# The normed tile of the second pass: turned by VectorE after a trip through memory, two units later

## The chip, the cores and the metric

The kernel runs on one core of a Trainium2 chip. A core has five engines with instruction queues of their own: TensorE (PE; its weight loads are shown apart, as PEld), VectorE (DVE), ScalarE (ACT), GpSimd (POOL) and SyncE (SP), which here only issues DMAs. Each queue is worked off in order; between queues there are semaphores. The metric is device time in microseconds (us); the profile is one execution of the same program, recorded by the hardware.

## The reference, cut to what matters

Two layers follow one another on an input of 8 images of 32 x 32 positions and 512 channels (f32). The first is a group norm, an attention over 1024 positions with 8 heads, and a residual. The second one is a deformable attention: a layer norm, a strided 7 x 7 depthwise convolution that gives sampling positions, 256 bilinear samples of the image as keys and values, attention of all 1024 queries over them, and then, for each position:

```python
msa = att @ mo_w + mo_b
z = msa + x.reshape(b, h * w, c)
z_ln = layernorm(z, ln_g, ln_b)
out = jax.nn.gelu(z_ln @ mlp_w + mlp_b, approximate=False) + z
```

The change concerns `z_ln @ mlp_w`. TensorE multiplies along the partition axis, so the normed tile, which has positions on the partitions, has to be turned until the channels lie there.

## The kernel before, in words

The program has two passes. The first does the first layer, the first layer norm and most convolutions; it ends near 2160 us of the profile. The second pass (`with ExitStack() as l1`) works in 64 units: `2 * B * NHP`, that is 16 half images `hi` (512 positions each) by 4 pairs of heads. Unit `n` computes the scores of its pair (`sc`), their maxima (`nmax`, VectorE), exponentials (`e`, ScalarE), turns `e` in blocks of 32 x 32 on VectorE (`sq`) and brings it to the form of `et` by a write to memory and a read; `att.product` (`av`) follows one unit later and `attH` holds the scaled result. `query_step` makes the queries of the next unit from `hat` (`hat_h`).

`back_steps(hi, start, step)` is the rest of a half image, as four tiles `t` of 128 positions, one tile per unit, in the units after the attention of that half. For each tile:

- `fetch`, `add` (per pair of tiles): read `xr` from `mid` (SP) and add `bo_row` (GpSimd)
- `joined`: product with `wo`, sum `z`, its mean and variance `mv` (VectorE; the power -1/2 on GpSimd, in `rstd`)
- `norm`: `zn`, VectorE
- `turned`: four 128 x 128 transposes on TensorE into PSUM, copied to `zT` by ScalarE in two halves
- `mlp`: product with `wm`, `zT` as weights; `biased`: `res`, VectorE
- `gelu` (ScalarE) and `end` (GpSimd: add `z`, write out), for two tiles together

The order is written out by hand: `at(place, step)` puts a step on a list, `run_due` runs the list in order of `place`, and `InOrder` keeps every engine's instructions in that order. The place is a unit and a fraction: 0 is the scores; 0.02 and 0.04 the two `sq` transposes with their writes; 0.0401 to 0.0411 the reads of `et` and `inv`; 0.042 the next queries; 1.1 and 1.2 `av` and `attH`. With `n` the unit of a tile, `turned` stood at n + 0.6, after the `av` of the unit before; `mlp` at n + 1.03, and the last steps of a pair at 1.72 and 2.24 behind its second tile.

Between these lie the remaining convolutions (`conv_steps`): lane 0 on VectorE (5 or 3 taps per unit), lane 1 on ScalarE and GpSimd (7 taps per unit: `parts`, then `chunk`), with `fill` products on TensorE. `point_steps(b)` turns the result of image `b` into positions (`targets`), gathers four rows per half (GpSimd, `row`, four buffers) and weighs them (`sample`, VectorE, `smp`), then makes keys and values of the image (`mm<-smp,wC`, `mm<-wB,smp`). With `NHP = 4` an image takes eight units.

Where the passes meet, `prep` loads `hat` twice, `lng` and `lnb` (`load_small`), repeats two vectors (`rep_w`, VectorE), gathers and samples image 0, loads the weights (`load_late`) and makes the first queries, keys and values. `rows` and `scaled` fold `lnb` and `lng` into `bm_row` and `wm`. DMAs of SP and of ScalarE take eight semaphores in turn; a DMA is issued when the eighth before it has landed.

Of the kernel before, what the change touches and what calls it, by code (L numbers as in the profile page):

```python
# [17 lines left out]
P = 128  # L18
# [229 lines left out]
def attention_then_deformable_attention(  # L248
# [131 lines left out]
    def at(place, step):  # L380
        due.append((place, len(due), step))
# [671 lines left out]
    with ExitStack() as l1:  # L1053
# [15 lines left out]
        def load_small():  # L1069
            with nc.allow_non_contiguous_dma(reason="small vectors onto partitions"):  # L1070
                for t, v in ((lng, ln_g), (lnb, ln_b)):
                    nc.sync.dma_start(t, v.rearrange("(c p) -> p c", p=P))

        def load_conv():
            nc.sync.dma_start(dww, dw_w.rearrange("(c p) a u v -> p c (a u v)", p=P))
# [94 lines left out]
        def fetch_hat(hi):  # L1170
            hat[hi] = raw.tile([P, NC, C], F32, tag="hat", name="hat_h", bufs=2)
            nc.sync.dma_start(hat[hi], hat_d[hi // 2][:, ts(hi % 2, NC), :])

# [29 lines left out]
        def back_steps(hi, start, step, tail=False):  # L1203
# [6 lines left out]

            def fetch(t):
                xr[t] = tmp("xr", 4)
                nc.sync.dma_start(xr[t], xs[t])

            def add(t):
                nc.gpsimd.tensor_tensor(xr[t], xr[t], bo_row, ALU.add)
# [9 lines left out]
                rstd(mv[:, 2:3], mv[:, 1:2], 1e-5)  # L1226

            def norm(t):
                zn[t], mv = tmp("zn", 2), xr["mv", t]
                nc.vector.tensor_scalar(  # L1230
                    zn[t], z[t], mv[:, 0:1], mv[:, 2:3], ALU.subtract, ALU.mult
                )

            def turned(t):
                ps = mm_tile()
                for c in range(NC):
                    nc.tensor.transpose(ps[:, ts(c, P)], zn[t][:, ts(c, P)], ident)
                zT[t] = tmp("zT", 2)
# [17 lines left out]
            for t in range(NC):  # L1256
                over, eve = (start + step * t >= n_units - i and not tail for i in range(2))
                n, pair = start + step * t, start + step * (t - t % 2)

                ends = (n + 0.6, n + 1.03, n + 1.0392)  # L1260
                if eve:
                    ends = (n + 0.61, n + 0.72, n + 0.73) if over else (n + 1.06, n + 1.62, n + 1.625)
                places = (pair - 1.6, pair - 0.5), (n + 0.012, n + 0.03), ends
                if tail:
                    turn = n + 0.15 + 0.005 * (t > 0)
                    places = (n - 0.7, n - 0.6), (n, n + 0.01), (turn, n + 0.25, n + 0.26)
                steps = (fetch, add), (joined, norm), (turned, mlp, biased)
                for place, what in zip(sum(places, ()), sum(steps, ())):
                    at(place, lambda t=t, what=what: what(t))


                ends = [t - 1, t] if t % 2 and not tail else [t] if tail else []

                for what, after in (
                    (gelu, 0.27 if tail else 0.735 if over else 1.72),
                    (end, 0.28 if tail else 0.74 if over else 2.24),
                ):
                    for i in ends:
                        at(n + after, lambda i=i, what=what: what(i))
# [33 lines left out]
        def conv_steps():  # L1313
            for lane, chunks in enumerate(((0, 3, 6), (1, 2, 4, 5, 7))):
                free = 0.5 + lane
                for k in chunks:
# [7 lines left out]
                    unit = int(fills[1]) + 1  # L1324
                    i = 0
                    while i < KS * KS:
                        points = unit % (2 * NHP) in (NHP - 1, NHP, NHP + 2)
                        count = 7 if lane else 3 if points else 5
                        for j in range(count):
                            if i == KS * KS:  # L1330
                                break
                            place = 0.25 + 0.01 * j if not lane else 0.045 + 0.001 * j if j < 4 else 0.65 + 0.01 * j
                            at(unit + place, lambda b=b, cb=cb, i=i, lane=lane: tap(b, cb, i, lane))
                            free = unit + place
                            i += 1
                        unit += 1

        def point_steps(b):
            last = 2 * NHP * b - NHP
            ready = last - (b == 1)  # L1340
            at(ready - 3.5, lambda: conv_load(b))
            at(ready - 2.035, lambda: conv_gelu(b))
            at(ready - 1.465, lambda: offsets(b))
            at(ready - 1.36, lambda: offsets_turned(b))
            at(ready - 0.959, lambda: targets(b))
            for h, (p0, p1) in enumerate(((-0.28, 0.0415), (1.72, 2.0415))):
                place = last if h else ready
                at(place + p0, lambda h=h: gather(b, h))
                at(place + p1, lambda h=h: sample(b, h))
# [6 lines left out]
        def load_late():  # L1356
            nonlocal bq_row, wo, wm, bo_row, bm_row, wq_r
            wo = load_w(late2, mo_w, "wo")
            wm = load_w(late2, mlp_w, "wm")
            bo_row = load_row(late, mo_b, "bo_row")  # L1360
            bm_row = load_row(late2, mlp_b, "bm_row")
            bq_row = load_row(wp, bq, "bq_row")
# [65 lines left out]
```

## Time and profile before

| | us |
|---|---|
| runs of the kernel before | 3321.34, 3324.23, 3326.19 (median 3324.23) |
| the profiled execution, own time | 3324.95 |
| its span, first to last instruction | 3323.3 |
| PE busy | 3263.3 (98%) |
| VectorE busy | 2494.1 (75%) |
| ScalarE busy | 1808.0 (54%) |
| GpSimd busy | 1540.5 (46%) |
| four transposes of zn, 64 times: PE busy | 41.9 |
| copies of zT, ScalarE busy | 41.0 |

All lines of the page have the line L54, a helper's, so work is told apart by tile names: `mm<-ident,zn` reads "writes mm, from ident and zn". A timeline row has the start, the duration, the engine, the operation, and in brackets how long the engine had been idle and what ended that. PE rows overlap by the pipeline, so a group's hold on PE is read from start to start. A table by stretches gives the busy time of each engine in a window. A list of waits gives who waited for whom, the total, the number of waits and the longest.

### The profile page before, as it was taken

What the parts mean: (1) busy time and instruction counts of PE and PEld (TensorE: products, weight loads), DVE (VectorE), ACT (ScalarE), POOL (GpSimd) and SP (SyncE); (2) the same over time, 40 slices, a digit from 0 to 9 for tenths busy, and PEclk for the clock granted to TensorE, in tenths of its full rate; (3) what the DMA queues carried; (4) which work ended last, traced back from release to release, by engine and by line L of the source; (5) the groups of instructions that cost most, each with busy time, mean ns of one, the idle gap of its engine ahead of it and who ended that gap; (6) DMA issues with size and microseconds to landing.
All of it is one profiled execution on the core that took longest, in us unless ns stands there. A gap on an engine that the chain in (4) does not pass through costs nothing.

```text
span 3323.3 us, 59497 instructions
## 1 busy us (share of the span) xinstructions
PE 3263.3 (98%) x21664; PEld 1323.2 (40%) x21664; DVE 2494.1 (75%) x3392; ACT 1808.0 (54%) x3918; POOL 1540.5 (46%) x1907
## 2 busy tenths in 40 slices
PE   8999999999999999999999999999999999999998
PEld 4344444444344344443444443333333333333333
DVE  5777777888898888888898787557767586665754
ACT  3443356576567567567567555145565565554442
POOL 1001316746755765664664663415555364641222
PEclk9999999999999999999999999999999999999999
DMA  5666766766767777776776776676666565675653
GB/s 151 178 178 164 210 179 186 217 190 177 220 192 185 207 201 186 204 196 179 211 199 171 201 214 189 178 240 211 198 197 214 175 214 187 202 231 191 214 182 130
DMA packets 442792, 643.62 MB, mean 194 GB/s; under 512 B 74274, under 2 KB 238114, under 8 KB 440452
## 3 DMA queue, kind: packets, MB, share of 16 engines
q1 hardware_dynamic: 409232, 531.93, 55.5%
q0 software_dynamic: 31632, 106.84, 10.6%
q8 instruction: 172, 2.82, 0.3%
q10 hardware_dynamic: 1636, 1.06, 0.1%
q14 instruction: 120, 0.98, 0.1%
HBM read 247.44 MB, written 123.74 MB: 112 GB/s over the span
## 4 chain that ended last, share of the span: by engine, by line
PE 88%; ACT 3%; DVE 3%; POOL 2%; DMA 1%; issue 1%; SPq 1%; another core or an unknown queue 0%; POOLq 0%; ACTq 0%; DVEq 0%
PE mm L54 55%; PE sc L54 17%; PE av L54 16%; ACT e L54 2%; SPq L54 1%; POOL chunk L54 1%; DVE nmax L54 1%; DVE smp L54 1%; DVE sq L54 1%; DMA et<-sq 0%; POOL xr L54 0%; POOL res L54 0%; ACT L54 0%; ACT parts L54 0%; DVE chunk L54 0%
## 5 line engine op out<-in xcount | busy, mean ns | idle before, releaser
L54 ACT ACTIVATE e<-sc,nmax 128x1024 f32<-128x1024 f32 (+1 forms) x1024 | 802.1, 796 | 477.6 <-DVE nmax L54 475.8
L54 DVE TENSOR_REDUCE nmax<-sc 128x1 f32<-128x1024 f32 (+1 forms) x640 | 751.3, 1214 | 347.1 <-PE sc L54 336.4
L54 POOL TENSOR_TENSOR oa<-part_x,oa 128x256 f32<-128x256 f32 x852 | 638.3, 749 | 549.7 <-ACT part_x L54 503.3
L54 DVE STREAM_TRANSPOSE sq<-e 128x1024 f32<-128x1024 f32 x640 | 766.1, 1228 | 157.0 <-ACT e L54 129.5
L54 ACT ACTIVATE part_x<-pad_x,dww_x 128x256 f32<-128x256 f32 x852 | 441.5, 545 | 258.1 <-POOL oa L54 256.8
L54 PE MATMUL sc<-k,q 64*64 64x512 f32 x4096 | 514.4, 603 | 10.7 <-ACT e L54 8.6
L54 PE MATMUL av<-et,v 128*64 128x256 f32 x4096 | 499.3, 386 | 7.3 <-DMA et<-sq 6.3
L54 PEld LDWEIGHTS av<-et,v 128*64 128x64 f32 x4096 | 272.9, 137 | 324.6 <-issue 164.0
L54 POOL TENSOR_TENSOR mv<-mv,minus_half 128x1 f32<-128x1 f32 x128 | 76.4, 597 | 461.0 <-DVE mv L54 460.2
L54 POOL TENSOR_TENSOR chunk<-parts,chunk 128x256 f32<-128x256 f32 x240 | 188.8, 787 | 197.9 <-ACT parts L54 183.8
L54 PEld LDWEIGHTS sc<-k,q 64*64 64x64 f32 x4096 | 139.1, 132 | 317.5 <-issue 208.2
L54 DVE SCALAR_TENSOR_TENSOR od<-pad_x,dww_x,od 128x256 f32<-128x256 f32 x276 | 233.2, 845 | 5.5
L54 PE MATMUL mm<-xT,wB 128*64 128x512 f32 x1024 | 233.6, 598 | 3.2 <-issue 3.2
L54 PE MATMUL mm<-wo,attH 128*64 128x512 f32 x1024 | 233.9, 598 | 1.3 <-DVE attH L54 1.3
L54 PE MATMUL mm<-wC,xT 128*64 128x256 f32 x2048 | 232.1, 379 | 0.0
L54 PE MATMUL mm<-wm,zT 128*64 128x512 f32 x1024 | 230.7, 592 | 1.0 <-ACT zT L54 1.0
L54 PE MATMUL mm<-hat_h,wA 128*64 128x512 f32 x1024 | 231.2, 594 | 0.0
L54 PE MATMUL mm<-xT,wA 128*64 128x512 f32 x1024 | 230.7, 592 | 0.0
L54 PE MATMUL mm<-w,attT 128*64 128x512 f32 x1024 | 230.1, 592 | 0.0
L54 ACT ACTIVATION_READ_ACCUMULATOR e<-sc,nmax 128x1 f32 x1024 | 209.3, 204 | 0.0
L54 ACT ACTIVATE parts<-pad,dww 128x256 f32<-128x256 f32 x240 | 126.5, 552 | 125.3 <-POOL chunk L54 124.4
L54 PEld LDWEIGHTS mm<-wC,xT 128*64 128x64 f32 x2048 | 147.6, 137 | 78.1 <-issue 6.4
(188 smaller groups left out, 3480.2 us busy)
## 6 DMA issues: line engine op xcount, KB each, us to landing
et<-sq SPq DMA_DIRECT2D x2048, 128.0 KB
sq_d<-sq SPq DMA_DIRECT2D x128, 512.0 KB
et<-sq_d SPq DMA_DIRECT2D x128, 512.0 KB
inv<-rs_d SPq DMA_DIRECT2D x256, 128.0 KB
hat_h<-hat_d SPq DMA_DIRECT2D x16, 1024.0 KB
xr<-mid SPq DMA_DIRECT2D x64, 256.0 KB
xr<-in_x_dram POOLq DMA_DIRECT2D x62, 256.0 KB
x<-in_x_dram POOLq DMA_DIRECT2D x60, 256.0 KB
```

What stands on the lines that cost most here:

```text
L54: return self.tc.keep_in_program_order(op(*args, **kwargs))
```

## The change

For 57 of the 64 tiles `turned` gives way to three steps. `away` writes `zn` to memory by one DMA (four pieces of 128 channels per position); `back` reads it so that a partition holds four neighbouring positions of one block of 128 channels; `blocks` turns it in blocks of 32 x 32 by one VectorE instruction. Channels end up on the partitions in another order (`(r c i)`, not `(c p)`), so `wm`, `lng` and `lnb` are loaded in that order, in four loads each, and the 7 tiles that are still turned by TensorE are normed into that order. `mlp`, `biased`, `gelu` and `end` come a unit later. `zn` and `zT` have one buffer each, the new tile `l` two.

Moved besides: the reads of `xr` go from SP to GpSimd and a unit forward; those of `hat` go to GpSimd in four parts; lane 0 has 7 or 2 taps per unit; the positions of the images 2 to 7 are computed a unit earlier, and the two gathers and samples have new places.

```diff
                 for t, v in ((lng, ln_g), (lnb, ln_b)):
-                    nc.sync.dma_start(t, v.rearrange("(c p) -> p c", p=P))
+                    for r in range(NSQ):
+                        nc.sync.dma_start(
+                            t[ts(r, SQ)], v.rearrange("(r c i) -> r i c", r=NSQ, c=NC)[r]
+                        )
...
+        def fetch_part(hi, c):
+            if c == 0:
+                hat[hi] = raw.tile([P, NC, C], F32, tag="hat", name="hat_h", bufs=2)
+            nc.gpsimd.dma_start(hat[hi][:, c, :], hat_d[hi // 2][:, hi % 2 * NC + c, :])
...
             def fetch(t):
                 xr[t] = tmp("xr", 4)
-                nc.sync.dma_start(xr[t], xs[t])
+                nc.gpsimd.dma_start(xr[t], xs[t])
...
+            def by_matmul(t):
+                return tail or start + step * t >= n_units - 2
+
+            def zn_tile(t):
+                return tmp("l", 2) if by_matmul(t) else tmp("zn", 1)
...
+            def away(t):
+                zn["d", t] = dram.tile([NSQ, P, P], F32, tag="zn_d", name="zn_d", bufs=3)
+                nc.sync.dma_start(
+                    zn["d", t].rearrange("r p x -> p r x"), zn[t].rearrange("p (r x) -> p r x", r=NSQ)
+                )
+
+            def back(t):
+                zn["l", t] = tmp("l", 2)
+                nc.sync.dma_start(
+                    zn["l", t], zn["d", t].rearrange("r (q k) x -> (r q) (k x)", k=NSQ)
+                )
+
+            def blocks(t):
+                zT[t] = zT_tile(t)
+                nc.vector.transpose(
+                    zT[t].rearrange("p (c q k) -> p k c q", c=NC, q=SQ),
+                    zn["l", t].rearrange("p (k c i) -> p k c i", k=NSQ, i=SQ),
+                )
...
-                ends = (n + 0.6, n + 1.03, n + 1.0392)
+                ends = (n + 0.0415, n + 1.001, n + 2.013, n + 2.05, n + 2.15)
+                if n == n_units - 2 and not tail:
+                    ends = (n + 1.055, n + 1.112, n + 1.16)
...
-                places = (pair - 1.6, pair - 0.5), (n + 0.012, n + 0.03), ends
+                places = (pair - 2.6, pair - 1.45), (n + 0.012, n + 0.03), ends
...
-                    (gelu, 0.27 if tail else 0.735 if over else 1.72),
-                    (end, 0.28 if tail else 0.74 if over else 2.24),
+                    (gelu, 0.27 if tail else 0.735 if over else 1.72 if n == n_units - 2 else 2.72),
+                    (end, 0.28 if tail else 0.74 if over else 2.24 if n == n_units - 2 else 2.95),
...
-                        points = unit % (2 * NHP) in (NHP - 1, NHP, NHP + 2)
-                        count = 7 if lane else 3 if points else 5
+                        points = unit % (2 * NHP) in range(NHP - 1, NHP + 3)
+                        count = 7 if lane else 2 if points else 7
...
-            ready = last - (b == 1)
-            at(ready - 3.5, lambda: conv_load(b))
...
-            for h, (p0, p1) in enumerate(((-0.28, 0.0415), (1.72, 2.0415))):
+            at(last - 4.5, lambda: conv_load(b))
...
+            at(last - 1.959, lambda: targets(b))
+            for h, (p0, p1) in enumerate(((-1.4, -0.959), (0.0125, 1.041))):
...
-            wm = load_w(late2, mlp_w, "wm")
+            wm = late2.tile([P, NC, C], F32, tag="wm", name="wm")
+            for r in range(NSQ):
+                nc.sync.dma_start(
+                    wm[ts(r, SQ)], mlp_w.rearrange("(r c i) o -> r i c o", r=NSQ, c=NC)[r]
+                )
...
-                at(NHP * (hi - 1) - (1.5 if hi == 2 else 1), lambda hi=hi: fetch_hat(hi))
+                for c, place in enumerate((-0.35, 0.65, 1.3, 1.65)):
+                    at(NHP * (hi - 1) + place, lambda hi=hi, c=c: fetch_part(hi, c))
```

More of the change, by code (lines that the diff above doesn't have):

```diff
@@ L1228, in norm, with zT_tile @@
             def norm(t):
-                zn[t], mv = tmp("zn", 2), xr["mv", t]
-                nc.vector.tensor_scalar(
-                    zn[t], z[t], mv[:, 0:1], mv[:, 2:3], ALU.subtract, ALU.mult
+                mv, to, src = xr["mv", t], zn_tile(t), z[t]
+                zn[t] = to
+                if by_matmul(t):
+                    to = to.rearrange("p (c r i) -> p r c i", r=NSQ, c=NC)
+                    src = src.rearrange("p (r c i) -> p r c i", r=NSQ, c=NC)
+                nc.vector.tensor_scalar(
+                    to, src, mv[:, 0:1], mv[:, 2:3], ALU.subtract, ALU.mult
+                )
[3 more added lines that the diff above has]
+                return tmp("l", 2) if by_matmul(t) else tmp("zn", 1)
+            def zT_tile(t):
+                odd = tail and t % 2 or not tail and start + step * t == n_units
+                return tmp("zn" if odd else "zT", 1)
+            def away(t):
[13 more added lines that the diff above has]
+                    zn["l", t].rearrange("p (k c i) -> p k c i", k=NSQ, i=SQ),
                 )
@@ L1237, in turned @@
                     nc.tensor.transpose(ps[:, ts(c, P)], zn[t][:, ts(c, P)], ident)
-                zT[t] = tmp("zT", 2)
+                zT[t] = zT_tile(t)
                 for half in range(2):
@@ L1266, in back_steps @@
                     places = (n - 0.7, n - 0.6), (n, n + 0.01), (turn, n + 0.25, n + 0.26)
-                steps = (fetch, add), (joined, norm), (turned, mlp, biased)
+                turns = (turned,) if by_matmul(t) else (away, back, blocks)
+                steps = (fetch, add), (joined, norm), (*turns, mlp, biased)
                 for place, what in zip(sum(places, ()), sum(steps, ())):
@@ L1339, in point_steps @@
             last = 2 * NHP * b - NHP
-            ready = last - (b == 1)
-            at(ready - 3.5, lambda: conv_load(b))
[L1342 to L1345, printed above, removed]
-            for h, (p0, p1) in enumerate(((-0.28, 0.0415), (1.72, 2.0415))):
-                place = last if h else ready
-                at(place + p0, lambda h=h: gather(b, h))
-                at(place + p1, lambda h=h: sample(b, h))
+            at(last - 4.5, lambda: conv_load(b))
+            at(last - 3.035, lambda: conv_gelu(b))
+            at(last - 2.465, lambda: offsets(b))
+            at(last - 2.36, lambda: offsets_turned(b))
+            at(last - 1.959, lambda: targets(b))
+            for h, (p0, p1) in enumerate(((-1.4, -0.959), (0.0125, 1.041))):
+                at(last + p0, lambda h=h: gather(b, h))
+                at(last + p1, lambda h=h: sample(b, h))
             first = 2 * NHP * b
```

## The prediction

> **What bounds the kernel now.** I read the busy table and the chain first, then stretches, then single units.
>
> ```profile
> PE 3263.3 (98%) x21664; PEld 1323.2 (40%) x21664; DVE 2494.1 (75%) x3392; ACT 1808.0 (54%) x3918; POOL 1540.5 (46%) x1907
> PE 88%; ACT 3%; DVE 3%; POOL 2%; DMA 1%; issue 1%; SPq 1%; another core or an unknown queue 0%; POOLq 0%; ACTq 0%; DVEq 0%
> ```
>
> TensorE bounds the whole. The second pass starts near 2160 us; the table by stretches says whether it does so there (columns: PE, PEld, DVE, ACT, POOL busy, clock, DMA share, GB/s):
>
> ```profile
> 2500.00:2600.00 100.00, 96.97 (x612) 36.77 (x610) 78.24 (x128) 60.66 (x168) 52.07 (x61) 1.00 0.63 206
> 2800.00:2900.00 100.00, 96.78 (x598) 36.66 (x592) 67.09 (x117) 61.35 (x167) 57.14 (x68) 1.00 0.63 202
> 3000.00:3100.00 100.00, 100.00 (x642) 39.09 (x638) 54.28 (x96) 43.00 (x122) 25.29 (x27) 1.00 0.60 197
> ```
>
> PE is full at clock 1.00. From 2300 to 3260 its gaps add up to 10.8 us. One unit, PE's timeline (start, duration):
>
> ```profile
> 3066.36 1.96 PE L54 MATMUL sc<-keys,q 64*64 64x256 f32 x32
> 3068.24 3.65 PE L54 MATMUL mm<-wo,attH 128*64 128x512 f32 x16
> 3071.73 3.60 PE L54 MATMUL mm<-wm,zT 128*64 128x512 f32 x16
> 3075.16 3.60 PE L54 MATMUL mm<-hat_h,wA 128*64 128x512 f32 x16
> 3078.59 1.89 PE L54 MATMUL av<-et,vals 128*64 128x512 f32 x8
> 3080.41 0.66 PE L54 MATMUL mm<-ident,zn 128*128 128x128 f32 x4
> 3081.00 1.96 PE L54 MATMUL sc<-keys,q 64*64 64x256 f32 x32
> ```
>
> Start to start a unit is 14.64 us, and the four transposes hold PE for 0.585 us of it. VectorE in the same unit:
>
> ```profile
> 3072.01 0.69 DVE L54 TENSOR_TENSOR z<-mm,xr 128x512 f32<-128x512 f32 x1 [1.29 <-PE mm L54]
> 3073.68 0.15 DVE L54 TENSOR_SCALAR mv<-mv 128x1 f32<-128x1 f32 x1
> 3073.76 1.25 DVE L54 STREAM_TRANSPOSE sq<-e 128x1024 f32<-128x1024 f32 x1
> ```
>
> Last, who made PE wait in the steady stretch, and what SP waited for where the passes meet:
>
> ```profile
> PE mm L54 <- DVE res L54: 5.0, 4, 1.6
> PE mm L54 <- DVE zn L54: 4.2, 4, 1.2
> ```
>
> ```profile
> SPq L54 <- DMA row_b<-row_b: 28.7, 2, 19.4
> SPq L54 <- DMA col<-row_b: 16.6, 2, 9.5
> SPq L54 <- DMA hat_d<-hat: 11.0, 2, 9.0
> ```
>
> **The sum** is made on the profiled execution: 3324.95 us, span 3323.3; the median of the runs is 0.7 us below it, 3324.23.
>
> *1. Transposes leave PE.* 64 tiles are turned; in the changed order 7 of them (those of units 62, 63 and 64 and the four of the tail) stay on TensorE. 57 x 0.585 = **-33.3 us**, all on the path. ScalarE loses 57 x 2 x 0.37 us, off the path.
>
> *2. Old gaps.* The waits for zn (4.2) and res (5.0) hang on a tile being normed, turned and multiplied within a unit. That loop is cut and res moves behind the second sq transpose: **-9**. In the last unit PE now has the product of tile 61 besides tile 62's; it falls into two gaps there (1.41 us behind a VectorE mv, 1.75 us behind et): **-3**, bounds -3.2 and 0.
>
> *3. VectorE's block transpose.* It stands between mv and the first sq transpose. PE needs zT as weights: after sc, wo, hat the wm product would start 8.80 us into the unit, its weight load some 0.4 us sooner, so 3074.75 in the unit above; VectorE is free at 3073.76. So about 0.95 us is free. The row next to it is the sq transpose, 1228 ns for 1024 elements: half is 0.61. But the output here steps by 16 bytes. Rows with a step: the first tap writes or reads 256 elements in 344 ns (1.34 ns each) where zn takes 506 ns (its median) for 512 (0.99), a factor 1.36, so 0.8 us; I take that, **+3** for units where it is just late. Lower end 0.6 us, no cost. Upper end, the slowest stepped row, a tap at 845 ns per 256 elements: 1.69 us, (1.69 - 0.95) x 57 = +42; nearer is the full 1.23 us, +16.
>
> [...]
>
> *4. The trip.* In the changed order SP issues `away` behind both `inv` reads, some 16.5 us after the unit starts (inv is issued at 3081.52 in the unit above and takes 1.38), and `back` behind it, first thing of the next unit. A store of twice the size is back for its reader within 3.3 us (sq_d issued at 2960.64, the et that waits for it some 3.3 us later), so `back` goes at about 20 us. Behind it in SP's queue is sq_d of the next unit, wanted at 22.7: free. The tile is read at 35: free. Memory: 0.52 MB more per unit. At 197 GB/s and a share of 0.60 the full rate is 328 GB/s; a unit of 14.06 us would run at 0.74: hidden, et has some 10 us to spare. zn with one buffer is free again at 20, wanted at 23.
>
> *5. GpSimd gets the xr reads and the hat reads in four parts.* That is one xr read and one part per unit, 0.57 us each in the rows of its other reads; SP loses 0.5 us per xr. xr is also fetched and its add made a unit earlier, so the 8.7 us for which VectorE's z waited for POOL's xr go (inside step 2). Where POOL is half idle that is nothing. Where lane 1's taps run (units 3 to 41) it is not. Take the fifth of eight units: mv 0.55, four gathers 5.1, seven taps 5.6, two xr 1.2, hat 0.6, two res adds 2.6, two stores 1.2: 16.9 us in a unit of 14.06. The adds come last, since gelu moved behind them too, and z has four buffers: the z of the next unit is written into the one that the first add frees. I get the add's end 9.7 us into that unit, then z, stats, mv, block transpose 2.6 us: zT at 12.3, wanted at 8.4 to 8.8. 3.5 us x 4 such units (12, 20, 28, 36) = **+14**. Bounds: 0 if POOL is early, and 26 if the two units beside it are late as well (0.5 and 1.2 to 2.5 us by the same count, VectorE having the sample's 4 us in them).
>
> *6. Taps, points, samples.* conv_load to targets move a unit earlier (for images 2 to 7), which their sources, done long before, allow; on SP the o read passes six small DMAs that nobody waits for there. Lane 0 has 7 and 2 taps instead of 5 and 3: in eight units 36 instead of 34. Those with 7 (5 us) have 4 to 7 us of PE work after av (keys, values, fills), where they hide; samples now lie in units with 2. Nothing, and if a fill is absent, up to 2 us a time, inside the bound of 5.
>
> *7. The MLP a unit later at the start.* Unit 6 has no wm product, 3.4 us moved to the last unit. Units 3 and 4 show that a thin unit doesn't shrink to its PE work (7.2 us of work, 9.4 and 13.2 us): **+2**, bounds 0 and 4.
>
> *8. Where the passes meet.* lng and lnb become eight loads instead of two, wm four instead of one. SP's and ACT's DMAs share eight semaphores in turn; the SP waits above are the loads there waiting for the DMA eight before. lng waited for a col read, lnb for row_b, the second hat_h for a col, wo to bm_row for the four hat stores of ScalarE (2166.19 to 2169.81). In the changed order the six extra loads push the last parts of lnb behind those stores. VectorE repeats lnb (2157.28 now) ahead of the eight sample operations, and POOL's second four gathers wait for the rows that these free. So: last lnb load issued at 2170.3 and landed 1.2 us later (row_b: issued 2147.98, waiter freed 2149.18), 2171.5; or 2167.2 if the stores land sooner without the traffic that moves behind them. From the first sample operation to the last it took 12.3 us (2157.61 to 2169.93), 9.6 if the gathered rows meet less traffic. Samples done 2177 to 2184 instead of 2169.93, and the key products wait for them: **+11**, bounds 7 and 14. All of the second pass starts later by that. [...]
>
> -33.3 - 9 - 3 + 3 + 14 + 2 + 11 = -15.3: 3309.6 for the profiled execution, **3309** for the median.
>
> **Rivals.**
> *Everything hidden* (POOL's adds in time, transpose within its 0.95 us, lnb at its lower bound): -33.3 - 10.8 - 3 + 7 = -40: 3285. For it: POOL is at 52 to 57% in its busiest stretches. Against: the 16.9 us count.
> *Slower: the block transpose is late in every unit.* Place: before the wm weights. From a duration d it costs 57 x (d - 0.95); the rest sums to -18.3, so it decides from d = 1.27, and passes +0.2% at 1.39. At 1.69 us it gives 3324 - 18 + 42 = 3348. For it: stepped taps are that slow. Against: they have two inputs, and get slow beside POOL's adds.
> *The z buffers run late in every gelu unit with taps*, 17 instead of 4: 17 x 3.5 = 60 in place of 14, 3355. Against: only one unit in eight has gathers and hat part together with the adds.
> *The gain is eaten* by 5 and 8 at their upper ends: -15.3 + 12 + 3 = 0, 3324.
>
> **How the numbers follow.** Forecast 0.50, everything hidden 0.18, gain eaten 0.13, late transpose 0.13, late z 0.06. Measurement tells about 0.2% (6.6 us) from no change. Faster: 0.50 and 0.18 less the forecast's upper edge, 0.67; same 0.13; slower 0.20. The forecast's own range is 3295 to 3320. For 8 in 10 I reach to the hidden case, 3286, and above into the late transpose at 1.2 to 1.4 us, 3332.
>
> **What would show it.** Step 1: PE's unit at 14.06 us where no taps run (after 3000). Step 3: the zT row at 0.6 to 0.95 us and no PE wait for zT there. Step 5: PE waiting 3 us for zT once in eight units, with VectorE's z waiting for POOL's res. Step 8: VectorE idle before rep_w<-lnb until about 2170, PE idle before smp,wC for some 12 us. I am wrong if the zT row is over 1.2 us, if POOL's reads stall its queue elsewhere, or if lnb lands in time.

## The result, and the profile after

The changed kernel is slower: 3348.66 us, median of four runs (3347.46 to 3355.6), against 3325.21 for the kernel before (3321.34 to 3327.12), a ratio of 1.0074 with a 95% interval of 1.0061 to 1.0087. Put beside other kernels on another chip later, it came out at 1.0060 [1.0045, 1.0075]. The prediction had 3309 and a range up to 3332.

The profiled execution took 3349.76 us, its span is 3347.7. The page's busy table and the shares of the chain:

```profile
PE 3248.8 (97%) x21436; PEld 1313.6 (39%) x21436; DVE 2536.7 (76%) x3449; ACT 1777.4 (53%) x3804; POOL 1602.5 (48%) x2027
PE 83%; DVE 5%; DMA 5%; SPq 2%; ACT 2%; issue 2%; POOL 1%; ACTq 0%; DVEq 0%; POOLq 0%
```

PE has 228 matmuls fewer (57 tiles by four), yet its busy time fell by only 14.5 us where 33 left; its share of the chain fell from 88% to 83%, and VectorE and the DMAs took that up. The same two stretches as before, and the one where the passes meet (columns: PE, PEld, DVE, ACT, POOL busy, clock, DMA share, GB/s):

```profile
2160.00:2260.00 100.00, 82.24 (x488) 31.35 (x484) 48.24 (x83) 32.59 (x97) 21.79 (x22) 0.90 0.65 202
2500.00:2600.00 100.00, 93.86 (x550) 34.82 (x548) 82.56 (x136) 54.50 (x148) 62.51 (x77) 0.98 0.76 239
3000.00:3100.00 100.00, 96.42 (x586) 36.64 (x586) 60.80 (x106) 42.97 (x126) 31.65 (x39) 0.98 0.71 225
```

PE was full after 3000; now it idles 3.6 us there and its mean clock is 0.98. Cut by the trace into three parts (units are counted from 0, by the first scores of each on PE), the 24.4 us of longer span lie here:

| | before | after | difference |
|---|---|---|---|
| start to the first scores of the second pass | 2183.81 | 2201.22 | +17.4 |
| first to last scores of the second pass (units 0 to 62) | 1073.91 | 1073.93 | 0.0 |
| last scores to the end | 65.5 | 72.5 | +7.0 |

Of the first line 1.5 us are the first pass (the repeat of `bvv`, the last thing ahead of the meeting, starts at 2158.48 instead of 2156.94) and 15.9 the meeting. The middle line is where the gain should have been. A unit without late work has it, by PE's timeline:

```profile
3261.10 1.96 PE L54 MATMUL sc<-keys,q 64*64 64x256 f32 x32
3262.99 3.65 PE L54 MATMUL mm<-wo,attH 128*64 128x512 f32 x16
3266.47 3.60 PE L54 MATMUL mm<-hat_h,wA 128*64 128x512 f32 x16
3269.90 3.60 PE L54 MATMUL mm<-wm,zT 128*64 128x512 f32 x16
3273.34 1.89 PE L54 MATMUL av<-et,vals 128*64 128x512 f32 x8
```

The next scores start at 3275.15: 14.05 us, 0.59 less than the 14.64 of before. Other units give it back. Who made PE wait from the meeting to the end, and then who made VectorE wait in the second pass (total, number, longest):

```profile
PE mm L54 <- DVE zT L54: 28.5, 16, 3.7
PE mm L54 <- DVE smp L54: 14.7, 2, 11.3
```

```profile
DVE z L54 <- POOL res L54: 27.6, 10, 5.4
DVE zn L54 <- DMA zn_d<-zn: 26.9, 17, 7.1
```

Between 2300 and 3260 PE's waits were 10.7 us before; in the same part of the pass they are 29.6 now, 25.4 of them for `zT`.

**Unit 45, the store of zn.** SP, VectorE and PE in one timeline:

```profile
2987.11 0.60 SPq L54 DMA_DIRECT2D zn_d<-zn  x1
2987.57 1.23 DVE L54 STREAM_TRANSPOSE sq<-e 128x1024 f32<-128x1024 f32 x1
2993.50 0.34 SPq L54 DMA_DIRECT2D l<-zn_d  x1
2993.58 0.55 DVE L54 TENSOR_SCALAR zn<-z,mv 128x512 f32<-128x512 f32 x1 [4.78 <-DMA zn_d<-zn]
3001.72 0.68 DVE L54 TENSOR_TENSOR z<-mm,xr 128x512 f32<-128x512 f32 x1
3003.45 1.08 DVE L54 STREAM_TRANSPOSE zT<-l 128x512 f32<-128x512 f32 x1
3004.67 5.35 PE L54 MATMUL mm<-wm,zT 128*64 128x512 f32 x16 [2.22 <-DVE zT L54]
```

The store of unit 44's tile is issued at 2987.11, 22.1 us after the first scores of that unit, and lands 6.4 us later, when its read can go out. VectorE wants the same buffer at 2988.8 for unit 45 and stands still for 4.78 us. Behind it in its order are `rs`, the second `sq`, the sample (2995.53 to 2998.26), `res`, `attH` and the maxima of the next unit; so the next unit's `z` and `zT` are late, and PE waits 2.22 us. The product that follows takes 5.35 us instead of 3.60; the mean granted clock over it (3004.67 to 3010.02) is 0.68, and 1.00 in the 10 us behind it.

**Where the passes meet.** VectorE and PE in the timeline:

```profile
2169.64 0.43 DVE L54 COPY rep_w<-lnb 128x512 f32<-128x512 f32 x1 [10.73 <-DMA lnb<-in_L_conv_ln_b_dram]
2178.44 0.49 DVE L54 TENSOR_SCALAR smp<-row,wt 128x512 f32<-128x512 f32 x1 [5.61 <-DMA row<-mid,ii]
2182.23 0.75 DVE L54 SCALAR_TENSOR_TENSOR smp<-row,wt,smp 128x512 f32<-128x512 f32 x1 [3.30 <-DMA row<-mid,ii]
2185.42 9.00 PE L54 MATMUL mm<-smp,wC 128*64 128x256 f32 x60 [11.33 <-DVE smp L54]
```

VectorE waits 10.73 us for the last `lnb` load, then 5.61 and 3.30 us for rows of the second gathers, which the first samples had held back. PE waits 11.33 us, and its first 60 products take 9.00 us at a mean granted clock of 0.76; without the wait (e2, below) they take 7.02.

**The tail.**

```profile
3283.78 3.65 PE L54 MATMUL mm<-wm,zT 128*64 128x512 f32 x16 [3.08 <-DVE zT L54]
3301.55 0.63 PE L54 MATMUL mm<-ident,l 128*128 128x128 f32 x4 [2.35 <-DVE l L54]
3302.11 5.35 PE L54 MATMUL mm<-wm,zT 128*64 128x512 f32 x16
```

The product of tile 61 came in, and two waits stand where two smaller ones (1.41 and 1.75 us) stood before.

### The profile page after: what moved, and what is told of

It reads as the page before. It is cut to its first block, busy times and chain, and to the rows that moved or that the text cites. A ratio compares the mean times of both kernels' runs of the same rounds, so it can differ in the third digit from the quotient of the medians.

```text
span 3347.7 us, 59193 instructions
## 1 busy us (share of the span) xinstructions
PE 3248.8 (97%) x21436; PEld 1313.6 (39%) x21436; DVE 2536.7 (76%) x3449; ACT 1777.4 (53%) x3804; POOL 1602.5 (48%) x2027
## 4 chain that ended last, share of the span: by engine, by line
PE 83%; DVE 5%; DMA 5%; SPq 2%; ACT 2%; issue 2%; POOL 1%; ACTq 0%; DVEq 0%; POOLq 0%
PE mm L54 51%; PE sc L54 16%; PE av L54 16%; DMA zn_d<-zn 2%; SPq L54 2%; DMA sq_d<-sq 1%; ACT e L54 1%; DVE sq L54 1%; DVE nmax L54 1%; DVE smp L54 1%; DVE chunk L54 1%; DMA et<-sq 0%; POOL chunk L54 0%; DVE zT L54 0%; DVE stats L54 0%
## 5 line engine op out<-in xcount | busy, mean ns | idle before, releaser
L54 PE MATMUL sc<-k,q 64*64 64x512 f32 x4096 | 514.2, 604 | 10.7 <-ACT e L54 8.7
```

The lines of the kernel that those rows point to most:

```text
L54: return self.tc.keep_in_program_order(op(*args, **kwargs))
```

## The experiments

Each kernel below is the changed one with the edit shown, except where the kernel before is named. Ratios are to the kernel before, run beside it on the same chip; over the five chips of these runs the kernel before has medians of 3327.06 to 3329.27 us, so the columns from the trace carry the finer comparisons. "Meeting" is the time from the repeat of `bvv` to the first scores, "pass" from the first scores to the last, "tail" from there to the end, all in us from the profiled execution. Two profiles of the changed kernel itself give the scatter: 42.7 and 41.4, 1073.9 and 1073.9, 72.5 and 72.5, with VectorE waiting 26.9 and 37.7 us for the store. e2 and e5, whose edits leave the pass alone, have 1073.7 and 1072.1, with 27.6 and 39.1 us. The totals of such lists are rough in another way too: a wait stands under the releaser that came last, so the 4.63 us that `z` of unit 21 waits in the changed kernel are put to PE and miss in the 27.6. Where it matters, single units are compared below.

| kernel | ratio, 95% interval | meeting | pass | tail |
|---|---|---|---|---|
| before | 1 | 26.9 | 1073.9 | 65.5 |
| changed | 1.0074 [1.0061, 1.0087] | 42.7 | 1073.9 | 72.5 |
| changed again (e0) | 1.0060 [1.0045, 1.0075] | 41.4 | 1073.9 | 72.5 |
| repeat of lnb behind the samples (e2) | 1.0018 [1.0003, 1.0033] | 26.7 | 1073.7 | 72.6 |
| before, lng and lnb in eight loads (e3) | 1.0033 [1.0020, 1.0046] | 40.2 | 1073.8 | 64.6 |
| zn in two buffers (e1) | 1.0025 [1.0011, 1.0039] | 42.2 | 1060.3 | 72.5 |
| store of zn sooner (e1b) | 1.0033 [1.0023, 1.0043] | 42.8 | 1060.4 | 72.9 |
| gelu and adds ahead of three taps (e4) | 1.0126 [1.0110, 1.0141] | 43.2 | 1100.5 | 73.8 |
| xr reads on SP (e8) | 1.0031 [1.0019, 1.0042] | 42.5 | 1065.9 | 71.9 |
| z in five buffers (e9) | 1.0069 [1.0054, 1.0085] | 42.1 | 1070.9 | 72.5 |
| fewer taps in two units (e12) | 1.0079 [1.0063, 1.0095] | 42.8 | 1084.5 | 72.8 |
| order of the last unit (e5) | 1.0041 [1.0028, 1.0054] | 42.5 | 1072.1 | 68.4 |
| e1, e2, e4, e5 (e7) | 1.0031 [1.0020, 1.0041] | 26.6 | 1081.4 | 68.6 |
| e1, e2, e5, e9 (e10) | 0.9959 [0.9944, 0.9974] | 26.6 | 1057.2 | 68.8 |
| and e8 (e11) | 0.9939 [0.9923, 0.9955] | 26.3 | 1054.2 | 67.3 |
| and e12 (e13) | 0.9901 [0.9883, 0.9919] | 26.7 | 1043.9 | 67.3 |
| with lane 0's fills apart (e14) | 0.9897 [0.9877, 0.9916] | 26.5 | 1043.8 | 67.3 |
| as that, zn in one buffer (e15) | 0.9984 [0.9973, 0.9996] | 26.6 | 1070.4 | 67.3 |

### Where the passes meet: e2 and e3

The first takes the wait from in front of the samples; the loads stay.

```diff
-            reps.extend(repeated(vec) for vec in (bvv, lnb))
+            reps.append(repeated(bvv))
...
                 gather(0, h)
                 sample(0, h)
+            reps.append(repeated(lnb))
```

> Base is the changed kernel. Edit: VectorE repeats lnb behind the eight sample operations of image 0, not ahead of them. The loads stay as they are. Theory (step 8: the repeat that waits for the last lnb load holds the samples, and these hold the second gathers, the key products and all of the second pass): VectorE's 10.7 us of idle time before the repeat goes, the last sample operation ends near 2171 instead of 2185, and the time falls by 13 to 18 us, to 3331 to 3336. Rival (the gathered rows and the weights are late by the traffic of the hat stores and of the weight loads anyway): the idle time comes back at the rows, and the time falls by less than 6.

Measured: the meeting is back at 26.7 us, and the time falls by 14 to 19 us by the ratios, as expected. VectorE and PE in its timeline:

```profile
2161.26 0.49 DVE L54 TENSOR_SCALAR smp<-row,wt 128x512 f32<-128x512 f32 x1 [1.57 <-DMA row<-mid,ii]
2171.72 0.43 DVE L54 COPY rep_w<-lnb 128x512 f32<-128x512 f32 x1 [2.35 <-DMA lnb<-in_L_conv_ln_b_dram]
2169.42 7.02 PE L54 MATMUL mm<-smp,wC 128*64 128x256 f32 x60 [1.37 <-DVE smp L54]
```

The last `lnb` load lands even later (15.2 us behind the repeat of `bvv` instead of 11.2), but nothing urgent waits for it; the first sample of the second rows starts 4.8 us behind that repeat instead of 20.0, and PE's first products are back at 7.02 us. So all of the meeting's cost hung on one VectorE instruction of 0.43 us in the wrong place.

The second adds that one thing to the kernel before (its order of channels stays).

```diff
                 for t, v in ((lng, ln_g), (lnb, ln_b)):
-                    nc.sync.dma_start(t, v.rearrange("(c p) -> p c", p=P))
+                    for r in range(NSQ):
+                        nc.sync.dma_start(t[ts(r, SQ)], v.rearrange("(c r i) -> r i c", r=NSQ, i=SQ)[r])
```

> Base is the kernel before (3325 us). Edit: only lng and lnb are loaded by eight DMAs (32 partitions each) instead of two; the order of channels stays that of the kernel before. It shows by itself what six more DMAs on SP cost where the passes meet. Theory (step 8): the last lnb load goes behind ScalarE's hat_d stores, VectorE waits before rep_w<-lnb until about 2169, and the time rises by 13 to 18 us, to 3338 to 3343. Rival (the meeting of the passes costs more in the changed kernel for another reason, the moved gathers or the four wm loads): it rises by less than 6.

Measured: +0.33% (11 us), below the 13 to 18 us expected but far from the rival's 6; the meeting is 13.3 us longer, the pass as before and the tail 1 us shorter. Six more small loads alone cost nearly all of what the meeting costs in the changed kernel (14.5 and 15.9 us in its two profiles); the four `wm` loads and the moved gathers can add 1 to 3 us.

### The store of zn: e1 and e1b

```diff
-                return tmp("l", 2) if by_matmul(t) else tmp("zn", 1)
+                return tmp("zn", 2)
...
-                return tmp("zn" if odd else "zT", 1)
+                return tmp("l" if odd else "zT", 1)
...
-                zn["l", t] = tmp("l", 2)
+                zn["l", t] = tmp("l", 1)
...
-                ends = (n + 0.0415, n + 1.001, n + 2.013, n + 2.05, n + 2.15)
+                ends = (n + 0.0415, n + 1.021, n + 2.013, n + 2.05, n + 2.15)
```

> Base is the changed kernel (3348.7 us). Edit: zn gets two buffers and l one; the read of l stands a little later in SP's queue (behind the first sq_d write of the next unit). Theory A (zn with one buffer makes VectorE wait for the store of the unit before, 26.9 us in 17 waits, and the rest of the unit's VectorE work with it): those waits go, PE's waits for zT (28.5 us) fall below 12, and the time falls by 10 to 22 us, to 3327 to 3339. Rival B (GpSimd: its late adds hold the z buffers, 27.6 us in 10 waits, and that alone makes zT late): zT waits stay above 20 us, the time falls by less than 4, to 3345 or more.

```diff
-                ends = (n + 0.0415, n + 1.001, n + 2.013, n + 2.05, n + 2.15)
+                ends = (n + 0.031, n + 1.001, n + 2.013, n + 2.05, n + 2.15)
```

> Base is the changed kernel. Edit: only the place of the store in SP's queue: zn_d is written right behind the first sq_d write (n + 0.031) instead of behind the inv reads (n + 0.0415), some 5 to 7 us sooner. Theory A1 (the store is issued too late; a landing of 4.6 to 6.2 us would do if it began sooner): VectorE's waits for zn_d go nearly to zero, and the time falls by 10 to 22 us, to 3327 to 3339, as with two buffers. Rival A2 (the store itself is what hurts: moved ahead of the et reads it makes et late): PE's waits for et grow from 5 us to over 15, and the time falls by less than 6.

Measured: both take VectorE's wait for the store away entirely, and in both the pass is 13.5 us shorter; by the ratios they save 9 to 16 us, according to which of the two results of the changed kernel they are set against. PE's waits for `zT` fell to 20.9 and 21.1, not below 12 as expected: there the rival was right, and a second cause is left. Who made PE wait with the sooner store:

```profile
PE mm L54 <- DVE zT L54: 21.1, 12, 3.8
PE av L54 <- DMA et<-sq_d: 3.4, 3, 1.9
```

PE's waits for `et` did not grow (5.4 in the changed kernel), so the store harms nobody ahead of the `et` reads; with one buffer, its place in SP's queue, behind the `et` and `inv` reads, was the harm. Most of what is left of the `zT` waits lies in the units 12, 13, 20, 21, 28, 29 and 37: there the third cause starts.

### GpSimd, ScalarE and z: e4, e8, e9, e12

```diff
-                    (gelu, 0.27 if tail else 0.735 if over else 1.72 if n == n_units - 2 else 2.72),
-                    (end, 0.28 if tail else 0.74 if over else 2.24 if n == n_units - 2 else 2.95),
+                    (gelu, 0.27 if tail else 0.735 if over else 1.72 if n == n_units - 2 else 2.63),
+                    (end, 0.28 if tail else 0.74 if over else 2.24 if n == n_units - 2 else 2.64),
```

> Base is the changed kernel (1.0074 of the kernel before). Edit: only gelu and the adds and stores behind it are moved up within their unit, from 2.72 and 2.95 to 2.63 and 2.64: ahead of the last three of lane 1's seven taps on ScalarE and GpSimd, not behind them. Theory (step 5: the adds come last, so z finds no free buffer, and zT is late in the units 13, 21, 29 and 37, 3.0 to 3.8 us each with 1.7 us of slower matmuls behind three of them): those waits go, VectorE's waits for GpSimd's res fall from 27.6 to under 8, and the time falls by 6 to 16 us, to 0.9975 to 1.0055 of the kernel before's. Rival (the store of zn holds the same units, so the z wait only hides behind it): it falls by less than 4.

Measured: 17 to 22 us slower than the changed kernel, by the ratios; the pass is 26.6 us longer. The waits aimed at did go (z for GpSimd's `res` 27.6 to 3.7 us; the units 13, 21, 29, 37 shrank by 3.1 to 3.3), but VectorE's waits for `e` rose from 8.6 to 48.8 us. The timeline of unit 21 shows how:

```profile
2561.28 1.32 POOL L54 TENSOR_TENSOR res<-res,z 128x512 f32<-128x512 f32 x1
2563.49 1.29 POOL L54 TENSOR_TENSOR res<-res,z 128x512 f32<-128x512 f32 x1
2566.97 0.54 ACT L54 ACTIVATE parts<-pad,dww 128x256 f32<-128x256 f32 x1 [4.58 <-POOL chunk L54]
2570.78 1.25 DVE L54 STREAM_TRANSPOSE sq<-e 128x1024 f32<-128x1024 f32 x1 [4.75 <-ACT e L54]
```

A tap of lane 1 goes ScalarE (`parts`, two buffers), GpSimd (`chunk`). With the adds ahead of the last three taps, ScalarE's last `parts` waits 4.58 us for GpSimd, and the exponentials stand behind it in ScalarE's order.

```diff
-                nc.gpsimd.dma_start(xr[t], xs[t])
+                nc.sync.dma_start(xr[t], xs[t])
```

> Base is the changed kernel. Edit: only the reads of xr go back to SP's queue, at their new places. It takes two issues (1.2 us) per pair of units from GpSimd. Theory (step 5 as the prediction had it: the reads given to GpSimd make its adds late): z waits for GpSimd's res fall by about 1.2 us per gelu unit that is late, and the time falls by 3 to 7 us. Rival (the adds are late because gelu stands behind seven taps that pass between ScalarE and GpSimd; two reads more or less hardly matter): the time falls by less than 3.

Measured: the pass 8.0 us shorter, 10 to 14 by the ratios, more than either side expected. In the units 13, 21, 29 and 37 `z` waits 3.54, 3.53, 3.52 and 5.03 us, against 4.63, 4.63, 5.39 and 4.48 in the changed kernel. So in three of the four the reads' own time on GpSimd, some 1.2 us, did come off, as the theory says, and there PE's wait for `zT` fell to 1.88 to 1.91 us, behind which the product took 3.65 us and was not slowed. `z` and the product of unit 21 in the changed kernel, then the product here, where `z` starts at 2561.08 after a wait of 3.53 us for GpSimd's `res`:

```profile
2558.20 0.69 DVE L54 TENSOR_TENSOR z<-mm,xr 128x512 f32<-128x512 f32 x1 [4.63 <-PE mm L54]
2561.16 5.35 PE L54 MATMUL mm<-wm,zT 128*64 128x512 f32 x16 [2.99 <-DVE zT L54]
```

```profile
2564.04 3.65 PE L54 MATMUL mm<-wm,zT 128*64 128x512 f32 x16 [1.88 <-DVE zT L54]
```

The units 13, 21 and 29 are 7.4 us shorter together. The waits for the store fell from 26.9 or 37.7 to 12.7 us, and the units 46, 53 and 54, which have no taps, are 6.5 us shorter; the units 30 and 37 give 6.0 us back. Why the store lands sooner with the reads on SP no run takes apart. On top of the other repairs, with two buffers for `zn`, the same move took 3.0 us out of the pass (e10 against e11).

```diff
-                z[t] = tmp("z", 4)
+                z[t] = tmp("z", 5)
...
-                res[t] = tmp("res", 3)
+                res[t] = tmp("res", 2)
```

> Base is the changed kernel. Edit: z gets five buffers and res two, nothing is moved. Theory (step 5's mechanism: z is late because GpSimd's adds free its buffer late): VectorE's waits of z for GpSimd's res, 27.6 us in 10 waits, go; the units 13, 21, 29 and 37 shrink by 2 to 4 us each, and the time falls by 6 to 14 us. Rival (there the zn store or VectorE's own work is just as late, so another wait takes its place): the waits of zn for its store grow by what z's lose, and the time falls by less than 4.

Measured: nothing gained (1.0069). The z waits for `res` are gone and the units 21 and 29 fell to 14.1 and 14.6 us, but the units after them grew: 20 to 22 take 49.6 us together, 49.8 and 50.6 in the two profiles of the changed kernel. The timeline of units 21 and 22 (ScalarE, GpSimd, VectorE) has the reason:

```profile
2552.42 3.29 POOL L54 TENSOR_TENSOR chunk<-parts,chunk 128x256 f32<-128x256 f32 x4
2557.34 2.39 POOL L54 TENSOR_TENSOR chunk<-parts,chunk 128x256 f32<-128x256 f32 x3
2559.99 1.15 ACT L54 ACTIVATE res<-res 128x512 f32<-128x512 f32 x2
2564.41 1.25 DVE L54 STREAM_TRANSPOSE sq<-e 128x1024 f32<-128x1024 f32 x1 [2.92 <-ACT e L54]
2577.97 0.67 DVE L54 TENSOR_TENSOR z<-mm,xr 128x512 f32<-128x512 f32 x1
```

GpSimd starts the taps of unit 20 only behind four gathers, at 2552.42. The gelu stands behind the seventh tap on ScalarE, the exponentials of unit 21 behind the gelu, with a table load (`ACT_TABLE_LOAD` in the trace, at 2558.69 and 2561.15) of 1.28 us on each side of it; VectorE waits 2.92 us, then has the sample (2567.74 to 2571.7) and two taps to do, and the `z` of unit 22 comes 10.9 us into that unit. So the chain is gathers, seven taps, gelu, exponentials or adds; more buffers, or adds moved up, only choose who waits at its end.

To shorten the chain itself, the next run takes taps out of it.

```diff
-                        count = 7 if lane else 2 if points else 7
+                        late = unit % (2 * NHP) - NHP
+                        count = (4 if late == 0 else 7) if lane else 0 if late == 1 else 2 if points else 7
```

> Base is the changed kernel (1.0060 to 1.0074 of the kernel before). Edit: only the number of taps per unit: lane 1 has 4 instead of 7 in the units 4 mod 8 (12, 20, 28, 36), lane 0 none instead of 2 in the units 5 mod 8; the taps left out follow later, so that both lanes end some two units later. Theory (what holds the stretches 20 to 22, 28 to 30 and 36 to 38 is the chain gathers, seven taps between ScalarE and GpSimd, gelu, adds; five buffers for z or earlier adds only move the wait to e and from there to the next unit's z): three units together shrink from 50 to 45 to 47 us, the z waits for GpSimd's res fall from 27.6 to under 16, and the time falls by 8 to 14 us. Rival (VectorE's sample operations, 4 us in one unit, are what make zT late): under 4 us.

Measured: 1.0079, no gain, and a pass 10.6 us longer. (Here and in e13 the fills of both lanes fall into unit 26 and share one product, so one chunk of image 7 is convolved from the wrong data; the work is the same in amount.) The chain did get shorter: in the units 13, 21, 29 and 37 `z` starts 5.7 to 6.5 us after the first scores instead of 8.8 to 9.8, and of these PE waits for `zT` in unit 29 alone, 0.5 us. But the units behind them grew: 22, 30 and 38 take 20.8, 21.5 and 21.8 us instead of 15.6, 15.7 and 14.6. The waits for the store of `zn` rose to 46.6 us, as its list of waits shows:

```profile
DVE zn L54 <- DMA zn_d<-zn: 46.6, 19, 6.2
DVE z L54 <- POOL res L54: 18.8, 11, 3.0
```

In unit 21 the norm waits 3.88 us for the store (until 2569.86) and then takes 3.47 us instead of some 0.5, beside GpSimd's adds of `bo_row`. Units 20 to 22 took 49.8 us. Taken alone, the expectation failed; what the run shows is that with `z` early the one buffer of `zn` is next. The two causes hide each other: with the buffer repaired and the taps left (e10, below) the units 22, 30 and 38 take 20.6, 22.1 and 16.1 us, with both repaired (e14) 15.6, 14.4 and 14.4.

### The tail: e5

```diff
+                if n == n_units - 3:
+                    ends = (*ends[:3], n + 2.105, n + 2.107)
                 if n == n_units - 2 and not tail:
-                    ends = (n + 1.055, n + 1.112, n + 1.16)
+                    ends = (n + 1.106, n + 1.112, n + 1.16)
                 if eve:
-                    ends = (n + 0.61, n + 0.72, n + 0.73) if over else (n + 1.06, n + 1.62, n + 1.625)
+                    ends = (n + 0.61, n + 0.72, n + 0.73) if over else (n + 1.06, n + 1.605, n + 1.607)
```

> Base is the changed kernel. Edit: order of TensorE's groups in the last unit alone: the product of tile 61 goes behind av of unit 62, the transposes of tile 62 behind that product, and the product of tile 63 ahead of the transposes of tile 64. Theory (step 2 went wrong there: the last product that came in is late by zT, 3.08 us, and the transposes of tile 64 wait 2.35 us for the norm and are followed by a slow product, 5.35 instead of 3.60 us): the first wait falls to about 1.3, the second goes with its slow product, and the stretch from the last scores to the end shrinks from 72.5 to 65 to 68 us; the time falls by 4 to 7 us. Rival (VectorE's chain through z, mv and norm sets the end of the tail): the waits come back at other groups and less than 3 us is gained.

Measured: 68.4 us instead of 72.5, just above the 65 to 68 expected, and no slow product in the tail. The first wait fell from 3.08 to 1.24; of the second 1.21 us came back at the transposes of a later tile.

### Together: e7, e10, e11, e13, e14, e15

> Four edits together on the changed kernel: two buffers for zn with one for l, the repeat of lnb behind the samples, gelu and adds ahead of the last three taps, the new order in the last unit. If the four costs are separate (about 14, 18, 10 and 5 us) they add up: 3349 - 47 = about 3302, 0.991 to 0.996 of the kernel before. If two of them hide each other (the zn and the z waits lie in the same units), 0.996 to 1.000.

> Four edits together on the changed kernel: two buffers for zn with one for l, the repeat of lnb behind the samples, five buffers for z with two for res, the new order in the last unit. By the traces of the single ones: meeting of the passes -16 to -18, second pass from 1074 to 1060 and by z another 8 to 12 less, tail -5: 3349 - 16 - 14 - 8 - 5 = about 3306, 0.992 to 0.997 of the kernel before. If z's wait only hides behind others: 0.997 to 1.000.

> As the kernel with four edits, and the reads of xr back on SP's queue. Theory (with z in five buffers GpSimd's adds are not waited for, and it no longer matters who issues the xr reads): within 2 us of the kernel with four edits. Rival (the reads on GpSimd also cost by their place among the other transfers: with xr back on SP the waits of zn for its store fell from 26.9 to 12.7 us): 4 to 10 us less than the kernel with four edits.

> The changed kernel itself, beside the next three on one chip, as the base of their differences. Both theories: slower than the kernel before by 0.5 to 0.9% (it was 1.0074 [1.0061, 1.0087]), that is 3340 to 3360 us, the meeting of the passes and the tail being the whole of it.

> The kernel with five edits (0.9939) and the taps of the run beside it. Theory as there: the units 22, 30 and 38, now 19.7, 19.7 and 16.5 us, fall to about 15, the second pass from 1054 to 1044, the time by 8 to 11 us to about 3300, 0.990 to 0.992 of the kernel before. Rival: they stay above 18 us and the time within 3 us of the kernel with five edits.

> The kernel with five edits and fewer taps where GpSimd is full: lane 1 has 4 instead of 7 in the units 4 mod 8, lane 0 none instead of 2 in the units 5 mod 8 and 9 instead of 7 in the units 0 mod 8, so that the fills of the two lanes stay in units of their own. Theory: as the run before it with nearly these taps, the units 20 to 22 take 44 to 45 us together, the second pass 1042 to 1046, the time 3295 to 3303, 0.989 to 0.992 of the kernel before. Rival: the two taps put into the units 0 mod 8 make zT late there, and it stays at 0.993 or more.

> As the run beside it, but zn with one buffer and l with two, and the read of l where the changed kernel has it: the price of step 4's wait when nothing else is late. Theory (the store of zn is on the path of VectorE in every unit that has other traffic): VectorE waits 25 to 45 us for the store, the second pass is 10 to 25 us longer than beside it. Rival (the waits were only long because z, the samples and the taps had already made VectorE late): less than 5 us longer.

With e4 in it the four edits give 1.0031 (its rise in the waits for `e` stays), outside of both ranges; with five z buffers in its place 0.9959, inside the range expected, and with the `xr` reads on SP 0.9939: by the ratios 7 us less, which is the rival's side. The taps, worth nothing alone, take another 10.3 us out of the pass there: 1043.9, 0.9901, as expected. e14 keeps the fills of the two lanes in units of their own and computes everything:

```diff
-                        count = 7 if lane else 2 if points else 7
+                        late = unit % (2 * NHP) - NHP
+                        count = (4 if late == 0 else 7) if lane else 0 if late == 1 else 2 if points else 9 if late == -NHP else 7
```

It takes 3295.73 us, 0.9897 [0.9877, 0.9916] of the kernel before and 1.6 to 1.8% less than the changed kernel by the ratios: better than both. Who made PE wait from 2300 to 3230 there, and then with one buffer for `zn` (and with it two for `l`, read where the changed kernel reads it), all else the same (e15):

```profile
PE mm L54 <- DVE zT L54: 6.3, 9, 1.3
PE mm L54 <- ACT th L54: 2.8, 6, 0.5
```

```profile
PE mm L54 <- DVE zT L54: 25.9, 14, 5.4
PE mm L54 <- ACT th L54: 2.8, 6, 0.5
```

One buffer costs 26.6 us of the pass, a little more than the 10 to 25 expected, and 29.5 us of the median: twice what e1 gave. 16.4 of the 26.6 us lie in the units 22, 30 and 38, the same that grew in e12, and that the late chain makes as long by itself: while it is there, each wait covers part of the other.

## Why the prediction was wrong, by its steps

The span was foreseen 15.3 us shorter and came out 24.4 us longer, 39.7 apart. In the pass the prediction had -33.3 - 9 + 3 + 14, and by step 7 another -3.4 (the product moved to the tail) + 2, so -26.7, and it was 0: 26.7. The tail was foreseen at about +0.4 (3.4 us of work in, 3 us of gaps out) and was +7.0: 6.6. The meeting was 15.9 instead of 11: 4.9. The rest, 1.5, is the first pass, and no part of the change.

Of the 26.7 us in the pass, e1 gives 13.6 to the one buffer of `zn` (step 4). The other 13.1 are, as an estimate from e1 and e14: 2.5 for the chain of gathers and taps (steps 5 and 6: 16.5 us between the two runs, where the sum had 14), 4.2 for the thin units, 3.3 for the block transpose, and 3.1 that stay open.

*1. Transposes leave PE: right.* Clean units are 14.05 us. With the stalls taken away (e14) the pass is 30.1 us shorter than before.

*2. Old gaps: half right.* The waits for `zn` and `res` of before (9.2 us) are gone. The tail's part was wrong: I let the product of tile 61 fall into two gaps, and did not follow when its `zT` is there. Unit 63 has no query product between `wo` and `wm`, so PE comes to it 3.08 us too soon. e5 shows 4.1 us of the 7.0 to be the order alone; e5 moves several groups at once, so how these divide is open.

*3. VectorE's block transpose: right in kind, low in size.* The row is 1.12 us in the median (1.07 to 1.17), 2.2 ns per element against 1.2 for `sq`; 0.8 was taken, 0.95 allowed free. In e14, where nothing else is late, nine waits for `zT` of 0.5 to 1.3 us are left, 6.3 in all; the step had +3 within 0 to 16. The factor of 1.36 taken from the stepped taps was an estimate; against half the `sq` row it was 1.8, and no run here shows its cause.

*4. The trip: the step that failed.* Two terms in it were best cases. "Some 16.5 us after the unit starts" was read from one quiet unit; by SP's timeline the 57 stores are issued 16.1 to 24.0 us after their unit's first scores, 18.0 in the median, behind `inv` and `et` reads that wait for stores of their own. "Back for its reader within 3.3 us" was one store too; `zn`'s land 4.3 to 9.4 us after the issue, 6.2 in the median (43 of the 57 have a landing on record), though they are half the size. So the buffer is free at 24.6 us in the median, not at 20, and wanted at 23 to 24 in a unit of 14 us: no room is left, and by VectorE's order each late `zn` makes the next `rs` and `sq` late, and by them the next store. The step saw that need and gave it 3 us from single rows. Price: 13.6 us of the pass on the changed kernel as it stands (e1; 13.5 in e1b), 26.6 with the other stalls gone (e14 against e15), none of it in the sum.

*5. GpSimd: the place and the size right, the mechanism only in part.* The units 13, 21, 29 and 37 have the late `z` that the step foresaw: it waits there 4.5 to 5.4 us, and PE waits for `zT` 3.02, 2.99, 3.75 and 2.83 us, 12.6 in all where the sum had 14. That three of the four products behind were slowed by some 1.7 us was not in it. By e8 the two reads given to GpSimd are 1.1 to 1.9 us of it in three of these units, and not in the fourth. e4, e9 and e12 show a chain through ScalarE which the step did not follow to its end: it had the gelu and the adds behind the taps, but not the exponentials behind the gelu. The step also thought of it as a cost to be added; e9 and e12 show that its removal alone brings nothing.

*6. Taps, points, samples: not nothing.* With the trip repaired, the seven taps of lane 1 in the unit of the gathers and the two of lane 0 in the unit behind it cost 10 us (e11 against e13 and e14).

*7. The thin unit: low.* Units 3 to 6 take 50.9 us instead of 49.3, though 3.4 us of work left them; with those 3.4 in the tail it is +5 instead of +2. In the other variants of the changed kernel these units take 48.6 to 52.1 us, whatever the edit, so the size is uncertain by about as much. PE waits there for `q` and `et`; no run took this apart.

*8. Where the passes meet: right, 5 us low.* The last `lnb` load was issued at 2167.4 and `lnb` was there at 2169.6, inside 2167.2 to 2171.5. The four loads took 1.9 to 2.3 us to land, not the 1.2 of the `row_b` row. The samples then took 15.4 us instead of 9.6 to 12.3, with waits of 5.61 and 3.30 us: the second gathers (from 2170.74) now come behind the weight loads (from 2168.49), at a DMA share of 1.05 from 2175 to 2185. PE's first products after the 11.33 us gap were 2 us slower. e2 and e3 show the cause from both sides; that the weight loads hold up the gathers is read from their places and not tested.

Among the rivals the slow ones were put on the transpose and on z. The one that took the place, `zn`'s buffer, was priced at nothing; that the late transpose gives 3348 at 1.69 us, the measured time, is chance, since its row is 1.12 us. "Everything hidden", 3285, is 11 us below e14 (3296), though e14 has none of the 7 us that this rival gave the meeting: not even with the stalls repaired does everything hide.

## What to carry to other kernels

When a tile that leaves by DMA has one buffer, take the landing from the slowest rows of such a store under the traffic of that place, since the next unit's whole queue stands behind it (here 4.3 to 9.4 us, where 3.3 had been taken). Before pricing a late engine, follow what is queued behind it on each engine it hands work to: taking away one of two waits in the same units moves the other into its place and measures as nothing. A small vector that is needed much later should not be read by an engine that has urgent work queued behind it, and a load cut into pieces can cost time though its bytes stay the same: `lng` and `lnb` in eight loads instead of two made the kernel before 11 us slower (e3).

## What the runs showed of the hardware that was not expected

*PE was slower behind most gaps above 2 us.* Over the 18 profiles I took the rows of 16 products (`wo`, `wm`, query) with an idle time above 0.4 us in front. A row at full speed takes 3.60 to 3.65 us. After gaps under 2.0 us none of 166 was slower; between 2.0 and 3.2 us 27 of 50 were; above 3.2 us 28 of 30. Most of the slower ones took 5.35 us, the slowest 6.65. Even the same gap differs: 2.99 us in one unit of the changed kernel gave 5.35, 3.02 in another 3.65. The mean clock in the stretches with such gaps is 0.90 to 0.98, and over the slow product of unit 46 it is 0.68. So a stall above 2 us cost in most cases 1.75 us again, and up to 3. The outcome depends on more than the length of the gap: 2.04 us was already enough once, and 3.08 us in the tail of the changed kernel was not. What else decides no run here shows.

*VectorE's norm stands still beside GpSimd's adds.* The norm of tile 64 takes 2.10 us at 3299.31, while GpSimd adds `bo_row` to `xr` from 3299.84 to 3301.1. It is most of the 2.35 us that PE waits for in the tail. Over the 18 profiles 891 norms with no add or tap of GpSimd beside them take 0.49 to 0.67 us, 0.51 in the median. Of 143 norms that start while such an instruction runs, 93 end 0.28 to 0.40 us after it does; the other 50, with the next one close behind, end 1.5 to 1.8 us after it. The kernel before has this too (1.07 us beside the adds to `res`), and in e12 it is 3.47 us beside two adds.
